# More tiles fetched row by row in a two-layer relational graph convolution: 119 instead of 95, with ScalarE taking part in layer 1

## The chip, the cores and the metric

The kernel runs on one core of a Trainium2 chip. The metric is device time in microseconds of one execution, as the median of several runs. The core has five engines with a queue each: TensorE (PE, with weight loads as PEld), VectorE (DVE), ScalarE (ACT), GpSimd (POOL) and SyncE (SP). DMAs are started here from the queues of SP, ACT and POOL.

## What is computed

12,500 nodes have 128 features each, and 200,000 edges, sorted by their target `dst`, have a source and one of eight types. A layer gives each node the sum over the types of the mean of its incoming messages of that type, adds the node's own product with `root` and a bias, and is followed by a relu and a residual. There are two such layers, and then a normalization of each row of `x + h`:

```python
W = jnp.einsum('rb,bio->rio', comp, basis)
xw = jnp.einsum('ni,rio->nro', x, W)
msgs = xw[src, et]
seg = dst * N_REL + et
mean = segment_sum(msgs, seg) / jnp.maximum(segment_sum(ones, seg), 1.0)[:, None]
agg = mean.reshape(N_NODES, N_REL, HIDDEN).sum(axis=1)
h_new = relu(agg + x @ root + bias)      # per layer; h = h_new + h
...
x = _layernorm(x + h, axis=-1)
```

## The kernel before

The edges are cut into 1563 tiles of 128, in the order of the targets; eight tiles make an octet, and there are 196 octets. Edge by edge, the row of the source has to come from HBM into a partition of its own: in layer 1 a row of `x` (512 bytes), in layer 2 a row of `y_d`, a table of every node's product with each of the eight type weights, which layer 1 writes as it goes (`table`, L1239; its stores are 512 KB each and leave from ACT's queue).

**How rows come.** Nearly every tile is fetched by one indirect DMA of POOL (`gather`, L687; the DMA is L707), which reads 128 rows by a column of indices. Seven octets of them fit into the ring `rows` (L558). `gathers` (L723) asks in iteration o for octet o + 5, and for the last six octets (`LATE`) only for octet o + 2, after PE has used the octet before (the `done` cell, L715). The other tiles, called lone here, are fetched by 128 plain DMAs of one row each, from SP's queue or ACT's (`lone_rows`, L641). These rows go in chunks of 32: one instruction loads 32 byte offsets into registers (L660), then 32 DMAs follow (L665). A chunk is due from 15 octets before its tile's octet (`EARLY`); SP issues in an iteration all that is due, ACT one chunk at most (the `break`, L671). The lists of lone tiles stand in L621 to L626: in layer 1 every 46th tile from 90 on by SP, 31 tiles; in layer 2 every 23rd from 44 on, by SP and ACT in turn, 32 tiles each. Layer 1's rows land in three buffers that are free by then (`jmp`, `comp_sb`, `sel`), layer 2's in four for each queue (the `sT` tiles); a chunk waits until PE has used the buffer's last tile. The byte offsets come from `load_offsets` (L675): two small loads on SP and three VectorE instructions in octet 1.

**What is done with them.** In layer 1, for each octet, VectorE builds one-hot matrices (`onehot`, L1030, line L1045), PE multiplies the rows by them (`means`, L1118, matmuls at L1128), ACT copies the result out (`take_means`, through `copy`, L608), PE multiplies by the weights (`product`) and places the result at its targets (`place`); between these, PE makes the table for layer 2, whose halves ACT copies out of PSUM (`y_row`, at L608). `batch` (L1419) gives ACT its work of an octet, right behind the octet's means. In layer 2, `add_rows` (L1278, matmuls at L1294) sums rows straight into blocks of 128 nodes. After every eight blocks `norm` (L1310) puts ten steps on a list, of which one is done per octet: turn, add x, statistics, a square root on ACT (L1347), scale, and a 512 KB store of the output on SP. When a block of eight begins its norm, the read of x for the block two further on, into the store's buffer, is put on the list behind the store (L1589), also on SP.

**What sets the order.** The program is a list of operations written out by hand, one loop iteration per octet. `Plan` turns reads and writes of named cells into semaphore waits. Each engine works through its own queue in order: a wait on SP or ACT holds everything behind it on that queue. A DMA into a buffer waits until the last reader and the last DMA of that buffer are done.

```python
while todo_ and todo_[0][0] // Q - EARLY <= q:
    t, j = todo_.pop(0)
    ...
    if e == "ACT":
        break
```

Of the kernel before, what the change touches and what calls it, by code (L numbers as in the profile page):

```python
# [422 lines left out]
def ordered_path(  # L423
# [25 lines left out]
    nc = tc.nc  # L449
# [28 lines left out]
    FIRST = 10  # L478
    TABLE = 50
    SOLO = 50  # L480
    ONE0, ONE_BY, CH, EARLY = 44, 23, 32, 15
    assert D == P and R * K == P and B == BF + 1 and 1 < TL and LAST < P and BF % 4 == 0 and Q == G and N % 2 == 0
    main = slice(HALO, HALO + P)

# [122 lines left out]
    def copy(out_t, in_t, reads, writes):  # L607
        act(lambda: nc.scalar.activation(out_t, in_t, AF.Copy), reads, writes)  # L608

    def in_turn(emits):  # L610
        def emit():
            for e in emits:
                last = e()
            return last

        return emit
# [1 line left out]
    rows_g = {}  # L618


    ones_at = list(range(ONE0, T - 8 * LATE - G, ONE_BY))  # L621
    single = [{t: ("SP", k) for k, t in enumerate(ones_at) if k % 2 == 0 and k > 0},
              {t: (("SP", "ACT")[k % 2], k) for k, t in enumerate(ones_at)}]
    turns_of = [{"SP": [], "ACT": []} for _ in range(L)]
    for l in range(L):
        for t in sorted(single[l]):  # L626
            turns_of[l][single[l][t][0]].append(t)
    offs = iota_f.bitcast(I32)
    byte = mybir.dt.uint8
    lone = {(0, "SP"): [(jmp.bitcast(F32), "jmp"), (comp_sb, "comp"), (sel.rearrange("p g k -> p (g k)"), "sel")]}  # L630
    for i, e in enumerate(("SP", "ACT")):
        f = sT_r.tiles[i].rearrange("p r g k -> p (r g k)")
        lone[1, e] = [(f[:, j * P:(j + 1) * P], ("sT", i, j // 4)) for j in range(4)]
    pending = {(l, e): [(t, j) for t in turns_of[l][e] for j in range(P // CH)] for l in range(L) for e in ("SP", "ACT")}

    def lone_tile(l, t):
        e, k = single[l][t]
        i = turns_of[l][e].index(t) % len(lone[l, e])
        return lone[l, e][i][0], [("lone", l, e, i, j) for j in range(P // CH)]

    def lone_rows(l, e, q):  # L641


        todo_ = pending[l, e]
        while todo_ and todo_[0][0] // Q - EARLY <= q:
            t, j = todo_.pop(0)
            k = single[l][t][1]
            o, cells = lone_tile(l, t)
            n = turns_of[l][e].index(t)
            writes = [cells[j]]  # L650
            if n < len(lone[l, e]) and j == 0:
                writes.append(lone[l, e][n][1])
            reads = [("offs", l)]
            if l == 1 and n == 0 and j == 0:
                reads += y_done
            table_b = (x if l == 0 else y_d).bitcast(byte).rearrange("n d -> (n d)")

            def emit(t=t, j=j, k=k, o=o):
                eng = nc.sync if e == "SP" else nc.scalar
                _, at = nc.values_load_multi_w_load_instructions(  # L660
                    offs[k:k + 1, l * P + j * CH:l * P + (j + 1) * CH],
                    engines=[mybir.EngineType.SP if e == "SP" else mybir.EngineType.Activation],
                    min_val=0, max_val=(N * (1 if l == 0 else R) - 1) * D * 4,
                    skip_runtime_bounds_check_because="the source of an edge is a node and its type a relation")
                return [eng.dma_start(o[j * CH + i:j * CH + i + 1, :].bitcast(byte),  # L665
                                      table_b[bass.ds(v, 4 * D)].rearrange("(p d) -> p d", p=1))
                        for i, v in enumerate(at)]

            plan.add(e, emit, reads, writes, lane="sr" if e == "SP" else "ar", n=CH)
            if e == "ACT":  # L670
                break  # L671
# [1 line left out]
    y_done = [("y_d", j) for j in range(NT - 2)] + [("y_d", j, k) for j in (NT - 2, NT - 1) for k in (0, 1)]  # L673

    def load_offsets():  # L675
        n = len(ones_at)
        for a, i in ((src, 0), (et, 1)):
            load(offs[:n, i * P:(i + 1) * P],
                 bass.AP(tensor=a.tensor, offset=a.offset + ONE0 * P, ap=[[ONE_BY * P, n], [1, P]]), [],
                 ["iota", ("offs", "raw", i)])  # L680
        a, b = offs[:n, :P], offs[:n, P:]
        vec(lambda: nc.vector.tensor_scalar(b, b, 4.0 * D, None, op0=ALU.mult), [], [("offs", "raw", 1)])
        vec(lambda: nc.vector.scalar_tensor_tensor(b, a, 4.0 * D * R, b, op0=ALU.mult, op1=ALU.add),
            [("offs", "raw", 0), ("offs", "raw", 1)], [("offs", 1)])
        vec(lambda: nc.vector.tensor_scalar(a, a, 4.0 * D, None, op0=ALU.mult), [], [("offs", "raw", 0), ("offs", 0)])

    def gather(l, q):  # L687
        if q >= NQ:
# [397 lines left out]
    def turn_x(n, h):  # L1086

        p, k = shape_of(n)
        pt, pc = pt_b
        m = min(4, k)  # L1090

        def first_step():
            t, c = xs[n]
            if h == 0:
                xT[n] = wide_r.take()

            def emit():
                for s in range(m):
                    last = nc.tensor.transpose(pt[:, s, :p], t[:p, 4 * h + s, :], ident[:p, :p])
                return last  # L1100

            pe(emit, [c, "ident"], [pc])

        def second_step():
            o, oc = xT[n]
            copy(by_slot(o, n)[:, 4 * h:4 * h + m, :], pt[:, :m, :p], [pc], [oc + (h,)])

        return first_step, second_step
# [9 lines left out]
    def means(o, half=None):  # L1118
        t, c = rows_g[0, o]
        d, dc = dms[0, o]  # L1120
        n = in_quad(o)

        lones = {i: lone_tile(0, o * Q + i) for i in range(n) if o * Q + i in single[0]}

        def some(i0, i1):
            def emit():
                for i in range(i0, i1):
                    last = nc.tensor.matmul(s_b[i // 4][0][:, i % 4, :], lones[i][0] if i in lones else t[:, i, :],  # L1128
                                            d[:, i, :], start=True, stop=True)
                return last  # L1130

            return emit

        if half is not None:
            pe(some(4 * half, 4 * half + 4), [c + (half,)] + dc, [s_b[half][1], ("done", 0)])
        else:
            pe(some(0, n), [c + (0,), c + (1,)] + dc + [x for _, cs in lones.values() for x in cs],
               [s_b[h][1] for h in range(-(-n // 4))] + [("done", 0)])
        plan.mark("PE")
# [99 lines left out]
    def table(j):  # L1239
# [5 lines left out]
        def half(k):  # L1245
            hb, bc = s_b[k] if j == NT - 2 else ct_b if split and k == 1 else pt_b

            def first_step():
                pe(lambda: nc.tensor.matmul(hb[:n].rearrange("p r d -> p (r d)"), hT[:, j * P:j * P + n],  # L1249
                                            w_sb[:, 1, k * H:(k + 1) * H, :].rearrange("p r d -> p (r d)"),  # L1250
                                            start=True, stop=True),
                   [("h", j)] + [("w", 1, r) for r in range(k * H, (k + 1) * H)], [bc])

            def second_step():
                if split and k == 1:
                    vec(lambda: nc.vector.tensor_copy(yr[:n, H:, :], hb[:n]), [bc], [yrc + (k,)])
                else:
                    copy(yr[:n, k * H:(k + 1) * H, :], hb[:n], [bc], [yrc + (k,)])
                if split:
                    load(y_d[j * P * R:(j * P + n) * R, :].rearrange("(p r) d -> p r d", r=R)[:, k * H:(k + 1) * H, :],  # L1260
                         yr[:n, k * H:(k + 1) * H, :], [yrc + (k,)], [("y_d", j, k)])
                elif k == 1:
                    stores.append(lambda: load(
                        y_d[j * P * R:(j * P + n) * R, :].rearrange("(p r) d -> p (r d)", r=R),
                        yr[:n].rearrange("p r d -> p (r d)"), [yrc + (0,), yrc + (1,)], [("y_d", j)], "ACT"))

            return first_step, second_step
# [10 lines left out]
    def add_rows(q, k, opens, last):  # L1278
# [8 lines left out]
            more += [hc, ("w", 1, R)]  # L1287

        lones = {i: lone_tile(1, q * Q + i) for i in range(n) if q * Q + i in single[1]}

        def some(i0, i1):
            def emit():
# [155 lines left out]
    for o in range(NG - 3):  # L1448
# [11 lines left out]
        onehot(0, o + 2, o - 1)  # L1460
        if parts is None:
            run(later, 1)
        if not opened:
            end()
        for step in opened:
# [19 lines left out]
        for i in range(2):  # L1485
# [4 lines left out]
            else:  # L1490
                break
            while copies:
                copies.pop(0)()
            a()
            if b is not None:
                copies.append(b)
# [69 lines left out]
    for q in range(NQ):  # L1566
# [15 lines left out]
        for i in range(2):  # L1582
            for j, step in ending:
                step()
                n = j // S
                if j >= 0 and (j % S == S - 1 or j == NT - 1):
                    norm(n)
                    if n + 2 < NX:
                        todo.append(lambda n=n: load_x(n + 2))  # L1589
            ending.clear()  # L1590
            if i == 0 and last:
                a, b = finish(1, k)
# [64 lines left out]
```

## Time and profile before

| What | us |
|---|---|
| median of 3 runs (lowest, highest) | 3869.61 (3868.55, 3869.77) |
| the profiled execution | 3870.23 |
| its span, first to last instruction | 3868.4 |
| layer 1, first to last gather of POOL | 4.3 to 1933.5 |
| layer 2, first to last gather of POOL | 1952.8 to 3848.6 |
| POOL busy, 3039 instructions | 2878.4 |
| PE busy | 2329.0 |
| VectorE busy | 1648.0 |
| ScalarE busy | 392.6 |

The span is 1.8 us shorter than the time of the execution that it belongs to. "Busy" leaves out the DMA issues and register loads of SP and ACT: SP never shows as busy, and ACT's share (10%) doesn't hold its single-row DMAs. Those are seen in the rows with "SPq" or "ACTq", in the list of DMA issues, and as packets of the DMA queues: q0 is POOL's gathers, q1 is SP's DMAs, q10 is ACT's. The chain of work that ended last goes back from the last instruction to whatever released each wait; an engine with a large share there is one that the end depended on.

### The profile page before, as it was taken

What the parts mean: (1) busy time and instruction counts of PE and PEld (TensorE: products, weight loads), DVE (VectorE), ACT (ScalarE), POOL (GpSimd) and SP (SyncE); (2) the same over time, 40 slices, a digit from 0 to 9 for tenths busy, and PEclk for the clock granted to TensorE, in tenths of its full rate; (3) what the DMA queues carried; (4) which work ended last, traced back from release to release, by engine and by line L of the source; (5) the groups of instructions that cost most, each with busy time, mean ns of one, the idle gap of its engine ahead of it and who ended that gap; (6) DMA issues with size and microseconds to landing.
All of it is one profiled execution on the core that took longest, in us unless ns stands there. A gap on an engine that the chain in (4) does not pass through costs nothing.

```text
span 3868.4 us, 57003 instructions
## 1 busy us (share of the span) xinstructions
PE 2329.0 (60%) x11213; PEld 1881.1 (49%) x11213; DVE 1648.0 (43%) x4646; ACT 392.6 (10%) x838; POOL 2878.4 (74%) x3039
## 2 busy tenths in 40 slices
PE   6767677777766676767755555555444354353446
PEld 4655555555555565655534444444334243242334
DVE  6654443333334333333233444443544353453445
ACT  1111112222111121221200000000000000000000
POOL 7777777777777777777767777777777777777775
PEclk8989889888888888888877777777777686776777
DMA  4122133333222222222222222222222222222222
GB/s 122 52 59 59 54 98 98 114 103 108 90 86 82 87 87 82 87 83 86 90 76 55 56 56 66 61 61 67 61 61 67 55 67 55 64 59 59 66 53 67
DMA packets 151007, 286.26 MB, mean 74 GB/s; under 512 B 64591, under 2 KB 84315, under 8 KB 150643
## 3 DMA queue, kind: packets, MB, share of 16 engines
q0 software_dynamic: 96992, 198.83, 19.9%
q10 hardware_dynamic: 25065, 54.12, 4.1%
q1 hardware_dynamic: 28586, 29.58, 2.8%
q14 instruction: 273, 2.24, 0.2%
q8 instruction: 91, 1.49, 0.2%
HBM read 223.63 MB, written 58.65 MB: 73 GB/s over the span
## 4 chain that ended last, share of the span: by engine, by line
POOL 47%; issue 19%; SPq 18%; DMA 7%; PE 5%; DVE 3%; ACT 0%; POOLq 0%; ACTq 0%; DVEq 0%
POOL rows L707 47%; SPq L665 14%; DMA rows<-y_d,idy 4%; SPq L660 4%; DMA out_dram<-x_g 2%; DVE dm L1045 2%; PE s L1294 1%; PE s L1128 1%; PE y L1160 1%; DVE arena L864 1%; DMA sT<-y_d 0%; PE ct L874 0%; PE ct L875 0%; PE ct L1294 0%; DMA rows<-in_x_dram,idx 0%
## 5 line engine op out<-in xcount | busy, mean ns | idle before, releaser
L707 POOL DMA_INDIRECT rows<-in_x_dram,idx x1532 | 1462.2, 954 | 469.3 <-issue 465.1
L707 POOL DMA_INDIRECT rows<-y_d,idy x1499 | 1415.1, 944 | 500.0 <-issue 446.7
L1045 DVE TENSOR_SCALAR dm<-cols,near,w 128x256 f32<-128x256 f32 x1563 | 723.7, 536 | 935.4 <-PE s L1294 515.1
L1294 PE MATMUL s<-dm,rows 128*128 128x256 f32 x2000 | 583.0, 447 | 422.9 <-DMA sT<-y_d 232.0
L1045 DVE TENSOR_SCALAR dm<-cols,kr,w 128x128 f32<-128x128 f32 x1563 | 526.7, 403 | 624.6 <-PE s L1128 460.3
L1128 PE MATMUL s<-dm,rows 128*128 128x128 f32 x3064 | 532.6, 343 | 410.1 <-DMA rows<-in_x_dram,idx 409.3
L1128 PEld LDWEIGHTS s<-dm,rows 128*128 128x128 f32 x3064 | 490.8, 250 | 526.4 <-DMA rows<-in_x_dram,idx 513.0
L1294 PEld LDWEIGHTS s<-dm,rows 128*128 128x128 f32 x2000 | 441.8, 229 | 531.5 <-issue 375.1
L1294 PE MATMUL ct<-dm,rows 128*128 128x256 f32 x998 | 308.2, 468 | 353.2 <-DMA sT<-y_d 177.5
L1294 PEld LDWEIGHTS ct<-dm,rows 128*128 128x128 f32 x998 | 232.3, 242 | 412.1 <-issue 310.3
L1160 PE MATMUL y<-w_sb,sT 128*128 128x128 f32 x1968 | 282.3, 304 | 44.3 <-ACT sT L608 44.3
L1160 PEld LDWEIGHTS y<-w_sb,sT 128*128 128x128 f32 x1968 | 270.8, 220 | 54.4 <-ACT sT L608 53.3
L608 ACT ACTIVATE sT<-s 128x512 f32<-128x512 f32 x391 | 213.4, 605 | 287.6 <-PE s L1128 287.6
L1249 PE MATMUL pt<-w_sb,arena 128*128 128x512 f32 (+1 forms) x386 | 203.4, 609 | 40.5 <-ACT y_row L608 39.2
L1209 DVE TENSOR_TENSOR v<-po,carry 128x128 f32<-128x128 f32 x98 | 28.5, 290 | 465.6 <-PE s L1128 279.7
L608 ACT ACTIVATE y_row<-pt 128x512 f32<-128x512 f32 x195 | 116.5, 597 | 1026.2 <-PE s L1128 902.0
L1347 ACT ACTIVATE st<-st,eps 128x8 f32<-128x8 f32 (+1 forms) x13 | 4.0, 308 | 1612.8 <-DMA sT<-y_d 1385.6
L1160 PE MATMUL ct<-w_sb,sT 128*128 128x128 f32 (+1 forms) x1168 | 164.5, 301 | 0.9 <-ACT sT L608 0.7
L1160 PEld LDWEIGHTS ct<-w_sb,sT 128*128 128x128 f32 (+1 forms) x1168 | 161.3, 220 | 1.7 <-ACT sT L608 1.7
L1191 PE MATMUL po<-pl,ys 128*128 128x256 f32 x392 | 126.8, 405 | 6.1 <-ACT sT L608 1.4
L1249 PEld LDWEIGHTS pt<-w_sb,arena 128*128 128x128 f32 (+1 forms) x386 | 63.0, 190 | 91.9 <-ACT y_row L608 87.9
L1053 DVE TENSOR_SCALAR pl<-cols,pos 128x256 f32<-128x256 f32 x196 | 93.3, 477 | 0.0
(151 smaller groups left out, 1077.3 us busy)
## 6 DMA issues: line engine op xcount, KB each, us to landing
sT<-y_d SPq DMA_DIRECT2D x4096, 0.5 KB
sT<-y_d ACTq DMA_DIRECT2D x4096, 0.5 KB
y_d<-y_row ACTq DMA_DIRECT2D x96, 512.0 KB
rows<-in_x_dram,idx POOLq DMA_INDIRECT x1532
rows<-y_d,idy POOLq DMA_INDIRECT x1499
jmp<-in_x_dram SPq DMA_DIRECT2D x1408, 0.5 KB
comp_sb<-in_x_dram SPq DMA_DIRECT2D x1280, 0.5 KB
sel<-in_x_dram SPq DMA_DIRECT2D x1280, 0.5 KB
```

The lines of the kernel that those rows point to most:

```text
L608: act(lambda: nc.scalar.activation(out_t, in_t, AF.Copy), reads, writes)
L660: _, at = nc.values_load_multi_w_load_instructions(offs[k:k + 1, l * P + j * CH:l * P + (j + 1) * CH], engines=[mybir.EngineType.SP if e = ...
L665: return [eng.dma_start(o[j * CH + i:j * CH + i + 1, :].bitcast(byte), table_b[bass.ds(v, 4 * D)].rearrange("(p d) -> p d", p=1)) for i, v ...
L707: ins.append(nc.gpsimd.indirect_dma_start(out=t[:, i - q * Q, :], out_offset=None, in_=x if l == 0 else y_d, in_offset=bass.IndirectOffset ...
L864: one = (lambda s=s, eq=eq, s0=s0: nc.vector.tensor_tensor(eq[:, s - s0, :nb, HALO - s:HALO + P], key[:, :nb, HALO - s:HALO + P], key[:, : ...
L1045: emits.append(lambda i=i: nc.vector.tensor_scalar(t[:, i - q * Q, :wide], cols[:, :wide], ids[:, i:i + 1], w[:, i:i + 1], op0=ALU.is_equa ...
L1053: emits.append(lambda: nc.vector.tensor_scalar(o[:m], cols[:m], pos[:m, g // (2 * R), g % (2 * R):g % (2 * R) + 1], None, op0=ALU.is_equal))
L1128: last = nc.tensor.matmul(s_b[i // 4][0][:, i % 4, :], lones[i][0] if i in lones else t[:, i, :], d[:, i, :], start=True, stop=True)
L1160: last = nc.tensor.matmul(y[:m], t[:, r, :nt, :].rearrange("p t k -> p (t k)"), w_sb[:, 0, r, :], start=(r == 0), stop=(r == R - 1))
L1191: ins = nc.tensor.matmul(a, o[:m], t[:m], start=opens, stop=last and not root_in)
L1249: pe(lambda: nc.tensor.matmul(hb[:n].rearrange("p r d -> p (r d)"), hT[:, j * P:j * P + n], w_sb[:, 1, k * H:(k + 1) * H, :].rearrange("p ...
L1294: ins = nc.tensor.matmul(a, lones[i][0] if i in lones else t[:, i, :], d[:, i, :], start=(opens and i == 0), stop=(last and i == n - 1))
```

## The change

The lists of lone tiles are written anew. Each queue has a first tile and a step for each layer, up to the end of octet 193. Layer 1 gets 34 tiles on SP (from 90, every 43rd) and 17 on ACT (from 498, every 64th); layer 2 gets 35 on SP (from 50, every 43rd) and 33 on ACT (from 53, every 46th). That is 119 tiles, and 3007 gathers of POOL are left of 3031.

- ACT's rows in layer 1 go 16 at a time, one chunk per octet, from 10 octets ahead of their tile. They are issued behind the octet's `batch`, once the preparation in `parts` is over. They land in two buffers in `mixer`.
- `load_offsets` now loads the two layers' offsets separately, six small loads instead of two, with `comp_sb` as a helper buffer for the types, and three VectorE instructions over other partitions.
- Where two copies fall into one octet of layer 1, the first is done by VectorE (`vcopy`) and not by ACT.
- The read of x in layer 2 comes four octets behind the output's store in the list of steps, where it came one octet behind.

```diff
-    ONE0, ONE_BY, CH, EARLY = 44, 23, 32, 15
+    EARLY = 15
...
+    def vcopy(out_t, in_t, reads, writes):
+        vec(lambda: nc.vector.tensor_copy(out_t, in_t), reads, writes)
...
-    ones_at = list(range(ONE0, T - 8 * LATE - G, ONE_BY))
-    single = [{t: ("SP", k) for k, t in enumerate(ones_at) if k % 2 == 0 and k > 0},
-              {t: (("SP", "ACT")[k % 2], k) for k, t in enumerate(ones_at)}]
+    LONES = (("SP", 90, 43), ("ACT", 62 * Q + 2, 8 * Q)), (("SP", 50, 43), ("ACT", 53, 46))
+    rows_at_once = {(0, "SP"): 32, (0, "ACT"): 16, (1, "SP"): 32, (1, "ACT"): 32}
...
+            ts = range(t0, (NQ - 2) * Q, by)
...
+    mixer_f = mixer.rearrange("p m k -> p (m k)")
+    lone[0, "ACT"] = [(mixer_f[:, j * P:(j + 1) * P], "mixer") for j in range(2)]
...
-        todo_ = pending[l, e]
-        while todo_ and todo_[0][0] // Q - EARLY <= q:
+        todo_, CH = pending[l, e], rows_at_once[l, e]
+        while todo_ and todo_[0][0] // Q - (10 if (l, e) == (0, "ACT") else EARLY) <= q:
...
     def load_offsets():
...
+        ty = comp_sb.bitcast(I32)
+        for l in range(L):
+            for p, t0, by, n in lists[l]:
+                for a, o, c in ((src, offs[:, l * P:(l + 1) * P], ["iota", ("offs", "raw", l)]),
+                                (et, ty, ["comp", ("offs", "ty")]))[:l + 1]:
+                    load(o[p:p + n, :], bass.AP(tensor=a.tensor, offset=a.offset + t0 * P, ap=[[by * P, n], [1, P]]),
+                         [], [c[0], c[1] + (p,)])
...
         if parts is None:
             run(later, 1)
+            lone_rows(0, "ACT", o)
...
             while copies:
-                copies.pop(0)()
+                copies.pop(0)(vcopy)
...
                     if n + 2 < NX:
-                        todo.append(lambda n=n: load_x(n + 2))
+                        todo.extend([lambda: None] * 3 + [lambda n=n: load_x(n + 2)])
```

More of the change, by code (lines that the diff above doesn't have):

```diff
@@ L618, in ordered_path @@
     rows_g = {}
-    ones_at = list(range(ONE0, T - 8 * LATE - G, ONE_BY))
-    single = [{t: ("SP", k) for k, t in enumerate(ones_at) if k % 2 == 0 and k > 0},
-              {t: (("SP", "ACT")[k % 2], k) for k, t in enumerate(ones_at)}]
-    turns_of = [{"SP": [], "ACT": []} for _ in range(L)]
+    LONES = (("SP", 90, 43), ("ACT", 62 * Q + 2, 8 * Q)), (("SP", 50, 43), ("ACT", 53, 46))
+    rows_at_once = {(0, "SP"): 32, (0, "ACT"): 16, (1, "SP"): 32, (1, "ACT"): 32}
+    single, turns_of, lists = [], [], []
     for l in range(L):
-        for t in sorted(single[l]):
-            turns_of[l][single[l][t][0]].append(t)
+        single.append({})
+        turns_of.append({})
+        lists.append([])
+        for e, t0, by in LONES[l]:
+            ts = range(t0, (NQ - 2) * Q, by)
+            lists[l].append((len(single[l]), t0, by, len(ts)))
+            turns_of[l][e] = list(ts)
+            for t in ts:
+                assert t not in single[l]
+                single[l][t] = e, len(single[l])
+        assert len(single[l]) <= P
     offs = iota_f.bitcast(I32)
@@ L633, in ordered_path @@
         lone[1, e] = [(f[:, j * P:(j + 1) * P], ("sT", i, j // 4)) for j in range(4)]
-    pending = {(l, e): [(t, j) for t in turns_of[l][e] for j in range(P // CH)] for l in range(L) for e in ("SP", "ACT")}
+    pending = {(l, e): [(t, j) for t in turns_of[l][e] for j in range(P // rows_at_once[l, e])] for l in range(L) for e in ("SP", "ACT")}
     def lone_tile(l, t):
         e, k = single[l][t]
+        assert not pending[l, e] or pending[l, e][0][0] >= t
         i = turns_of[l][e].index(t) % len(lone[l, e])
-        return lone[l, e][i][0], [("lone", l, e, i, j) for j in range(P // CH)]
+        return lone[l, e][i][0], [("lone", l, e, i, j) for j in range(P // rows_at_once[l, e])]
     def lone_rows(l, e, q):
-        todo_ = pending[l, e]
-        while todo_ and todo_[0][0] // Q - EARLY <= q:
+        todo_, CH = pending[l, e], rows_at_once[l, e]
+        while todo_ and todo_[0][0] // Q - (10 if (l, e) == (0, "ACT") else EARLY) <= q:
             t, j = todo_.pop(0)
@@ L675, in load_offsets @@
     def load_offsets():
[L676 to L685, printed above, removed]
+        ty = comp_sb.bitcast(I32)
[5 more added lines that the diff above has]
+                         [], [c[0], c[1] + (p,)])
+        n0, n = len(single[0]), len(single[1])
+        a, b, ty = offs[:n0, :P], offs[:n, P:], ty[:n, :]
+        raw = [[("offs", "raw", l, p) for p, _, _, _ in lists[l]] for l in range(L)]
+        tys = [("offs", "ty", p) for p, _, _, _ in lists[1]]
+        vec(lambda: nc.vector.tensor_scalar(a, a, 4.0 * D, None, op0=ALU.mult), [], raw[0] + [("offs", 0)])
+        vec(lambda: nc.vector.tensor_scalar(ty, ty, 4.0 * D, None, op0=ALU.mult), [], tys)
+        vec(lambda: nc.vector.scalar_tensor_tensor(b, b, 4.0 * D * R, ty, op0=ALU.mult, op1=ALU.add),
+            ["comp"] + tys, raw[1] + [("offs", 1)])
     def gather(l, q):
@@ L1102, in first_step, with second_step @@
             pe(emit, [c, "ident"], [pc])
-        def second_step():
+        def second_step(copy=copy):
             o, oc = xT[n]
@@ L1123, in means @@
         lones = {i: lone_tile(0, o * Q + i) for i in range(n) if o * Q + i in single[0]}
+        assert not any(p and p[0][0] < o * Q + n for p in (pending[0, "SP"], pending[0, "ACT"]))
         def some(i0, i1):
@@ L1252, in first_step, with second_step @@
                    [("h", j)] + [("w", 1, r) for r in range(k * H, (k + 1) * H)], [bc])
-            def second_step():
+            def second_step(copy=copy):
                 if split and k == 1:
@@ L1289, in add_rows @@
         lones = {i: lone_tile(1, q * Q + i) for i in range(n) if q * Q + i in single[1]}
+        assert not any(p and p[0][0] < q * Q + n for p in (pending[1, "SP"], pending[1, "ACT"]))
         def some(i0, i1):
```

## The prediction

> **What bounds the kernel now.** I read the chain of work that ended last, then the costliest groups, then the waits, then the DMA queues by stretches.
>
> ```profile
> POOL 47%; issue 19%; SPq 18%; DMA 7%; PE 5%; DVE 3%; ACT 0%; POOLq 0%; ACTq 0%; DVEq 0%
> ...
> L707 POOL DMA_INDIRECT rows<-in_x_dram,idx x1532 | 1462.2, 954 | 469.3 <-issue 465.1
> L707 POOL DMA_INDIRECT rows<-y_d,idy x1499 | 1415.1, 944 | 500.0 <-issue 446.7
> ```
>
> Two engines carry the chain: POOL, which issues a gather for nearly every tile, and SyncE's queue (SPq), which fetches the other tiles row by row. A gather of POOL costs 0.944 us and 0.305 us of issue: in layer 1 between 1000 and 1800 us, 640 of them filled 799.9 us, 1.249 us each. So a tile taken from POOL is worth 1.249 us, as long as POOL is what ends last.
>
> In layer 1 it is: POOL goes at that pace from 4.3 to 1933.5 us, and PE ends an octet's means 4 to 5 us behind the octet's last gather. In layer 2 (1952.8 to the end) it is only just so. POOL waits 25.4 us for PE from 3150 us on, because PE waits for rows:
>
> ```profile
> POOL rows L707 <- PE ct L1294: 13.4, 3, 5.5
> POOL rows L707 <- PE s L1294: 12.0, 4, 5.0
> ```
>
> The rows are what has no room in layer 2. Both issuing queues work without a break from its start nearly to its end (4096 rows each; times are of the first and last issue):
>
> ```profile
> L665 SPq DMA_DIRECT2D sT<-y_d x4096: 227/228/604, 1954.2 to 3771.7; - x196
> L665 ACTq DMA_DIRECT2D sT<-y_d x4096: 234/235/618, 1954.3 to 3706.0; - x196
> ```
>
> What limits them? SyncE's own waits show 115.9 us behind the output's store, which the change removes:
>
> ```profile
> SPq L605 <- DMA out_dram<-x_g: 115.9, 9, 16.4
> ```
>
> But the DMA queues say that issuing is not the limit. q1 is SyncE's, q10 ScalarE's; a row is two packets, 512 bytes and 4 bytes. First 2120 to 2320 us, in which SyncE doesn't stop, then 2327 to 2343 us, in which it waits for a store:
>
> ```profile
> q1 hardware_dynamic: 921, 0.24, 1.6%
> q10 hardware_dynamic: 891, 0.23, 1.2%
> ```
> ```profile
> q1 hardware_dynamic: 203, 0.54, 11.0%
> q10 hardware_dynamic: 69, 0.02, 1.0%
> ```
>
> The first pair is 906 rows in 200 us, **4.53 rows/us** for both queues together (2.30 and 2.23). In the second, less the store's 128 packets of 4 KB, it is 72 rows in 16 us, 4.5 rows/us, although SyncE issued none: a backlog was served. Early in the layer (1956 to 2056 us) 252 and 249 rows are issued and 466 moved, so the backlog grows, to some 12 us of rows in each queue; then an issue takes up to 604 ns instead of 227. When ScalarE is done (3710 to 3770 us), SyncE alone moves 354 packets, 2.95 rows/us. So the two queues share one pace, and SyncE's stops are mostly covered by what is queued.
>
> [...]
>
> **The change, part by part.** Base: the profiled execution, 3870.2 us with a span of 3868.4; the median of the runs, 3869.61, is 0.6 us less.
>
> *Fewer gathers.* Layer 1 goes from 31 single-row tiles to 34 + 17 = 51, layer 2 from 64 to 35 + 33 = 68. POOL issues 20 and 4 gathers less: 20 x 1.249 = **-25.0 us** and -5.0 us where POOL ends last.
>
> *Layer 2's rows.* There are 68 x 128 = 8704 of them, not 8192. With SyncE no longer stopped, both queues stay at the shared pace: ScalarE needs 4224 / 2.23 = 1894 us, a few less for the faster start (466 rows per 100 us), say 1890. SyncE has moved 2.30 x 1890 = 4347 by then; the other 133, at its lone issue pace (154 rows in 60 us), take 52 us. Its last row is issued some 1940 us after its first; before, that took 3771.7 - 1954.2 = 1817.5. Its last tile, 1512, lies in octet 189, and the gathers of octets 192 to 195 wait for PE to have used it: 27 x 1.249 = 34 us, 5 us for landing and matmuls, and 3868.4 - 3848.6 = 20 us from the last gather to the end. So layer 2 lasts about 1940 + 59 = 1999 us from its first row, against 3868.4 - 1954.2 = 1914: +85. It is less if both queues end together at the pace of the whole layer: by 3700 us some 8030 rows were out in 1746 us, 4.60/us, so 8704 / 4.60 + 59 = 1951, +37. POOL, held up, also leaves the DMAs freer: where it issued 37 gathers in 50 us (3360 to 3410), 475 row packets were moved, 4.75 rows/us. I take **+75**, near the upper end, because ScalarE's share can't pass to SyncE before it ends.
>
> *The read of x, three octets later.* The store and the load have 4 chunks of 32 rows between them in SyncE's queue, over 50 us, so the nine stops go. Cover: the next block's sum needs that read an interval of 16 octets later (turns at 2312 and 2468 us). Nothing else stands behind it but rows. Its worth at a shared pace is 0 to -10 us (the pace falls from 4.53 to about 4.3 for 40 us around a store); taken as 0, inside the +75.
>
> *ScalarE's 16 rows an octet in layer 1.* From octet 52 on, an octet lasts (8 - 0.31) x 1.249 = 9.6 us. ScalarE's work in it: copies 1.75 us (1200.04 to 1201.78), a table store 0.34, 16 rows at 249 per 100 us with their load, 6.4, or up to 7.6 if the register load stays at 2.26 us for half the rows (one register takes 0.46). Sum 8.5 to 9.7: it just fits, or loses 0.1 x 130 octets = 13 us, within the 55 us between PE's last use of a rows buffer and the gather that fills it again (octet 184's means end at 1834.7 us, octet 191's gather starts at 1890.0). The queued work behind it is the next `take_means`, for which PE waits; a delay stays in that room until it is used up.
>
> *Layer 1's rows together.* SyncE: 128 per 43 tiles, 41.3 x 1.249 = 51.6 us, 2.48/us; ScalarE 16 / 9.6 = 1.67/us; 4.15 together, under 4.53, but with 96 table stores of 512 KB on ScalarE's queue. A SyncE tile took 53 us in 518 to 1262 us, against 51.6: it loses 1.5 us a tile over 25 tiles, 37 us. Its lead at 518 us, with nine tiles fetched: the tenth, 477 in octet 59, would be there at 571 us, and PE is at octet 56 at 579.7, three octets short, so at 609: 38 us. That is used up at the end. Bounds: 0 to +60. I take **+5**.
>
> *The small ones.* Some 76 copies (62 of `y_row`, 14 of `wide`, those that made ScalarE wait for PE inside an octet) go to VectorE: 0.6 to 1.1 us each beside a VectorE that is idle over half of layer 1 and waits for the same matmuls; 0. Were that cover gone, 76 us at most. Four more loads of offsets on SyncE at 2 us each (45.90 to 49.88 us for the two now) hold VectorE and the first rows by 8 us in octet 1, where POOL's ring has room (octet 2's means end at 63.8 us, octet 9's gather starts at 97.0); 0.
>
> **Sum**: 3870.2 - 25 + 5 + 75 = 3925 us. Layer 2's four gathers give nothing, since POOL isn't last there.
>
> **Rivals.**
> *Faster.* SyncE's stops, not the pace, hold layer 2. Then 140 chunks of 12.7 us (its pace right after a stop, 2343 to 2420) are 1780 us, POOL ends last, its 25 us of waits go too: 3870.2 - 25 - 5 - 23 = **3817**. For it: the nine stops lie on the chain. It decides at 4.8 rows/us: 8704 rows by octet 189's gathers, 1453 x 1.249 = 1815 us. Against: 4.53 to 4.75 in every stretch, stops included. Anything between ends about level.
> *Slower still, layer 1.* The pace binds there too, as the stores take DMA time: SyncE at 2.30 rows/us needs 55.7 us a tile, 25 x 4.1 = 103 us behind demand, less 38 of lead: +65 in place of +5, **3985**. For it: from 520 us on SyncE has at most 38 us of lead and must now win none. Against: x's rows were fetched alone without a sign of backlog.
> [...]
> *The change doesn't do what it says*: the read still finds the store unfinished. Then SyncE stops 116 us in sum and ends up to 40 us later, near 3960.
>
> **Chances.** Forecast 0.56, layer 1 binding too 0.15, stops remaining 0.05; faster 0.20; level 0.04. Within 0.2% (8 us, about what a measurement of this kernel can tell from no change): 0.04; faster 0.20; slower 0.76. The range, 3850 to 3985, leaves out about 0.14 below and 0.05 above; the slower cases alone lie within 3890 to 3985.
>
> **What would show it.** Right: POOL's gathers 3007 at 944 ns, but some 75 us or more of waits for PE in layer 2; no wait of SPq for `out_dram<-x_g`; SPq's rows of `sT` ending about 100 us nearer the layer's end; packets of q1 and q10 at 4.5 to 4.75 rows/us through layer 2, 906 to 950 per 200 us; layer 1 ending near 1910 to 1915 us. Wrong: more than 4.8 rows/us, or POOL without waits in layer 2 (then the faster rival); POOL waiting for PE before 1900 us (then layer 1's).

## The result, and the profile after

| | before, us | after, us |
|---|---|---|
| median (lowest, highest), 4 runs each | 3869.08 (3868.18, 3869.77) | 3911.43 (3910.33, 3913.71) |
| the profiled execution, its span | 3870.23, 3868.4 | 3911.06, 3908.9 |
| layer 1, first gather to end of the last | 4.3 to 1933.5 | 4.6 to 1908.0 |
| layer 2, first gather to the end of the span | 1915.6 | 1984.1 |
| POOL's waits for PE in layer 2 | 26.9 | 103.5 |

The ratio is 1.011 (95%: 1.0093 to 1.0128): the change makes the kernel slower, by 42 us where 55 were forecast. The experiments fell on several chips, which differ: on one of them, called A below, the kernel before takes 3869.65 us, as it does here; on the four others, called B, it takes 5757 to 5833 us. Which chip the table's runs had is not on record; since their times for the kernel before are 0.6 us apart, they are compared with chip A's. Each experiment is compared with runs of the kernel before on its own chip.

The page's chain of work that ended last, and its two largest groups (busy us, mean ns of one | idle before, and what ended most of it):

```profile
POOL 35%; SPq 31%; issue 19%; ACTq 6%; PE 4%; DMA 2%; DVE 2%; ACT 1%; POOLq 0%; DVEq 0%
...
L726 POOL DMA_INDIRECT rows<-y_d,idy x1495 | 1411.2, 944 | 570.6 <-issue 440.2
L726 POOL DMA_INDIRECT rows<-in_x_dram,idx x1512 | 1442.4, 954 | 463.7 <-issue 458.3
```

A gather takes what it took, 944 ns, and there are 3007. But the chain has moved to SyncE's queue: its share goes from 18% to 31%, and POOL's falls from 47% to 35%. In layer 2 POOL now idles 570.6 us, of which only 440.2 lie between gathers.

The two row queues in layer 2, from the list of DMA issues by line (ns min/median/max; first and last issue):

```profile
L679 SPq DMA_DIRECT2D sT<-y_d x4480: 227/228/632, 1926.7 to 3849.2; - x195
L679 ACTq DMA_DIRECT2D sT<-y_d x4224: 234/235/597, 1926.8 to 3781.2; - x192
```

SyncE issues its last row 1922.5 us after its first, and the span ends 59.7 us later; before, it was 1817.5 us. SyncE hardly stops meanwhile. Its own waits from 1920 us on, and POOL's there (us in total, times, longest):

```profile
SPq L605 <- DMA out_dram<-x_g: 5.3, 1, 5.3
```
```profile
POOL rows L726 <- PE s L1315: 79.0, 14, 14.9
POOL rows L726 <- PE ct L1315: 24.5, 5, 8.2
```

The nine stops behind the output's store, 115.9 us, are gone, as the change means them to be, and the queue ends later all the same. Why the end depends on that queue is seen in the last part of the chain in order of time (start, duration, what):

```profile
3836.95 2.10 SPq L674
3849.16 1.18 DMA sT<-y_d
3850.47 1.19 PE s L1315 x2
3851.66 0.43 PE s L1318 x2
3852.09 4.10 PE s L1315 x14
3856.45 0.94 POOL rows L726
```

SyncE loads the last 32 offsets at 3837, its last row lands at 3850, PE uses the tile, and only then may POOL gather the last four octets: 27 gathers and 20 us, to 3908.9.

Last, the DMA queues from 2120 to 2320 us (packets, MB, share of 16 engines):

```profile
q1 hardware_dynamic: 1064, 0.76, 2.3%
q10 hardware_dynamic: 892, 0.23, 1.2%
```

q1 holds 128 packets of a 512 KB block besides the rows. Without them it is 936 + 892 packets, 914 rows in 200 us, 4.57 rows/us; in the same stretch it was 906 before. The pace did not rise.

### The profile page after: what moved, and what is told of

It reads as the page before. It is cut to its first block, busy times and chain, and to the rows that moved or that the text cites. A ratio compares the mean times of both kernels' runs of the same rounds, so it can differ in the third digit from the quotient of the medians.

```text
span 3908.9 us, 63322 instructions
## 1 busy us (share of the span) xinstructions
PE 2252.7 (58%) x11213; PEld 1811.6 (46%) x11213; DVE 1684.7 (43%) x4714; ACT 346.9 (9%) x770; POOL 2854.7 (73%) x3015
## 4 chain that ended last, share of the span: by engine, by line
POOL 35%; SPq 31%; issue 19%; ACTq 6%; PE 4%; DMA 2%; DVE 2%; ACT 1%; POOLq 0%; DVEq 0%
POOL rows L726 35%; SPq L679 24%; SPq L674 6%; ACTq L679 5%; ACTq L674 1%; PE s L1148 1%; DMA rows<-y_d,idy 1%; DVE dm L1064 1%; PE s L1315 1%; PE y L1180 1%; DMA rows<-in_x_dram,idx 1%; ACT sT L608 1%; PE ct L893 0%; DVE arena L883 0%; PE ct L894 0%
## 5 line engine op out<-in xcount | busy, mean ns | idle before, releaser
L726 POOL DMA_INDIRECT rows<-y_d,idy x1495 | 1411.2, 944 | 570.6 <-issue 440.2
L726 POOL DMA_INDIRECT rows<-in_x_dram,idx x1512 | 1442.4, 954 | 463.7 <-issue 458.3
L1315 PE MATMUL s<-dm,rows 128*128 128x256 f32 x2004 | 566.3, 437 | 619.0 <-DMA sT<-y_d 365.7
L1315 PEld LDWEIGHTS s<-dm,rows 128*128 128x128 f32 x2004 | 430.3, 223 | 723.0 <-issue 443.7
L1148 PE MATMUL s<-dm,rows 128*128 128x128 f32 x3024 | 496.5, 328 | 295.9 <-DMA rows<-in_x_dram,idx 286.5
L1148 PEld LDWEIGHTS s<-dm,rows 128*128 128x128 f32 x3024 | 458.7, 237 | 413.5 <-DMA rows<-in_x_dram,idx 372.2
L1315 PE MATMUL ct<-dm,rows 128*128 128x256 f32 x986 | 277.4, 434 | 294.3 <-DMA sT<-y_d 162.7
L1315 PEld LDWEIGHTS ct<-dm,rows 128*128 128x128 f32 x986 | 210.7, 222 | 345.7 <-issue 246.0
L1269 PE MATMUL pt<-w_sb,arena 128*128 128x512 f32 (+1 forms) x386 | 215.5, 642 | 45.9 <-DVE y_row L611 43.9
L611 DVE COPY y_row<-pt 128x512 f32<-128x512 f32 x56 | 38.7, 692 | 356.8 <-PE pt L1269 356.8
L608 ACT ACTIVATE y_row<-pt 128x512 f32<-128x512 f32 (+1 forms) x139 | 83.0, 597 | 1047.9 <-PE s L1148 669.6
L1211 PEld LDWEIGHTS po<-pl,ys 128*128 128x128 f32 x392 | 62.8, 195 | 136.1 <-ACT sT L608 129.2
```

Of the source, the lines that this page charges most:

```text
L611: vec(lambda: nc.vector.tensor_copy(out_t, in_t), reads, writes)
L726: ins.append(nc.gpsimd.indirect_dma_start(out=t[:, i - q * Q, :], out_offset=None, in_=x if l == 0 else y_d, in_offset=bass.IndirectOffset ...
L1211: ins = nc.tensor.matmul(a, o[:m], t[:m], start=opens, stop=last and not root_in)
L1315: ins = nc.tensor.matmul(a, lones[i][0] if i in lones else t[:, i, :], d[:, i, :], start=(opens and i == 0), stop=(last and i == n - 1))
```

## The experiments

**ScalarE's rows of layer 2 given back to POOL (chip A).**

```diff
-(("SP", 50, 43), ("ACT", 53, 46))
+(("SP", 50, 43), ("ACT", 9999, 46))
```

> The kernel after, with ScalarE's 33 single-row tiles of layer 2 given back to POOL (1528 gathers there, not 1495); layer 1 is unchanged. Theory (one shared pace for both row queues, and layer 2 too full for it): SP's 4480 rows alone ask for 4480 / 1908 = 2.35 rows/us, under the 4.6 that both reached together, so a chunk takes the 12.6 to 12.8 us of its issue and not the 13.7 it took in the kernel after; SP's last row then comes 140 x 12.7 = 1780 us after its first, POOL ends last and its waits for PE in layer 2 fall from some 98 us to under 30. Layer 2 lasts 1528 x 1.249 = 1908 us and the 40 around it; where the kernel before takes 3869 us this gives 3870 to 3885, faster than the kernel after although ScalarE's help is taken away. Rival (POOL's waits come from the block ends, with ScalarE's late square root, and not from the rows): the waits stay near 98 us, and the 33 gathers more add 41 us: 3950. On a chip where the kernel before takes some 5825 us, a tile by rows cost about 21 us of the queue against 1.25 us for a gather: SP alone then needs 140 chunks at 20 us or more, 2800 us in layer 2, near the 2925 that it took with both queues, since a chunk lost its time there to the gathers and not to the other queue.

Measured: 3856.55 us against 3869.65 for the kernel before, ratio 0.9967 (0.9954 to 0.9979). It beats both kernels. That is below the 3870 to 3885 us expected, but the theory's own terms, 1908 us of gathers from 1928.8 us on and 20 us behind them, add up to 3857: the expectation added them wrongly. Its chain, its group of layer 2's gathers, its row queue (from the list by line), its waits of POOL from 1920 us on, and q1 from 2120 to 2320 us:

```profile
POOL 66%; issue 22%; PE 4%; ACTq 4%; DVE 2%; DMA 2%; ACT 1%; POOLq 0%; SPq 0%; DVEq 0%
...
L729 POOL DMA_INDIRECT rows<-y_d,idy x1528 | 1442.8, 944 | 484.9 <-issue 465.8
```
```profile
L680 SPq DMA_DIRECT2D sT<-y_d x4480: 227/228/364, 1930.3 to 3730.8; - x195
```
```profile
POOL rows L729 <- issue: 465.8, 1527, 0.3
POOL rows L729 <- DMA y_d<-y_row: 19.2, 1, 19.2
```
```profile
q1 hardware_dynamic: 1144, 0.78, 1.2%
```

The same 4480 rows of SyncE take 1800.5 us instead of 1922.5, 12.9 us a chunk (12.6 to 12.8 were expected) and not 13.7, only because ScalarE issues none. In 200 us SyncE moves (1144 - 128) / 2 = 508 rows, 2.54/us, where it moved 468 beside ScalarE. The packets tell how. Taken from the trace by size, a row's 512-byte packet in these 200 us takes 25.7 ns on average; in the kernel after it takes 91.1 ns in q1 and 72.3 ns in q10, with a median of 27 ns against 25 here. So most packets go nearly as fast as alone (361 of q1's 460 in the kernel after take at most 30 ns), and others take far longer (88 of them 300 ns or more). POOL has no wait for PE left in layer 2, SPq is off the chain, and 33 more gathers, 41 us, make the span 52.4 us shorter. So ScalarE's 33 tiles cost layer 2 some 94 us and saved 41. What the rival says, that the late square root holds PE, the time of this run can't exclude: without its rows ScalarE takes the square root at once, and VectorE's wait for it falls from 245.1 us to 0.7. The two traces can, for SyncE's queue. Added up, its 4480 issues take 1029 us here and 1151 us in the kernel after, while the loads of offsets into registers (311 us) and the register move ahead of each issue (130 us in sum) are the same in both. The 122 us between the sums are the whole 122 us by which the queue ended later. Where something else held SyncE's queue, as the output's store did in the kernel before, the trace lists waits, 115.9 us of them; in layer 2 of the kernel after it lists 10 us in sum, and the issues are longer.

**Hardly any row tiles (chip A).**

```diff
-LONES = (("SP", 90, 43), ("ACT", 62 * Q + 2, 8 * Q)), (("SP", 50, 43), ("ACT", 53, 46))
+LONES = (("SP", 90, 700), ("ACT", 9999, 64)), (("SP", 50, 700), ("ACT", 9999, 46))
```

> The kernel after with only three single-row tiles in each layer (SP: 90, 790, 1490 and 50, 750, 1450), all others gathered by POOL: 3120 gathers, not 3007. Theory (a gather costs 1.249 us of POOL wherever nothing else is late): where the kernel before takes 3869 us, 3120 - 3031 = 89 gathers more than before, 111 us, less the 25 us of waits that POOL had in layer 2: 3955 to 3985, slower than the kernel after by 45 to 75 us. On a chip where the kernel before takes some 5825 us the theory says that row issues are held up by POOL's gathers, so without them it is POOL's pace alone: also 3955 to 4000, a third faster than the kernel before there. Rival for such a chip (everything is slow there, not the row issues alone): POOL's gathers would fall behind as well, and the time stays well over 5000 us.

Measured: 3953.25 us, ratio 1.0217 (1.02 to 1.0234), just under the range expected. From the list by line:

```profile
L729 POOL DMA_INDIRECT rows<-y_d,idy x1560: 940/944/1095, 1984.1 to 3931.1; - x195
L729 POOL DMA_INDIRECT rows<-in_x_dram,idx x1560: 940/944/1762, 4.4 to 1964.7; - x195
```

POOL alone sets the time: 1560 gathers in 1947 us in layer 2. Against the kernel after, layer 1's last gather starts 1964.7 - 1907.1 = 57.6 us later for 48 gathers, 1.20 us each: that is what a row tile is worth in layer 1. So row tiles do pay on chip A, as long as the queues can carry them; this kernel is 42 us slower than the kernel after, and 97 slower than the one with SyncE's rows alone in layer 2.

**The change in its two halves (chips B).** Layer 1's new lists alone, with layer 2's lists and the read of x as before; and layer 2's new lists with the later read, with layer 1's lists and copies as before. The layer that is as before also gets its old end of the list (not shown); `load_offsets` stays as changed in both:

```diff
-(("SP", 50, 43), ("ACT", 53, 46))
+(("SP", 44, 46), ("ACT", 67, 46))
...
-todo.extend([lambda: None] * 3 + [lambda n=n: load_x(n + 2)])
+todo.append(lambda n=n: load_x(n + 2))
```
```diff
-(("SP", 90, 43), ("ACT", 62 * Q + 2, 8 * Q))
+(("SP", 90, 46), ("ACT", 9999, 64))
...
-copies.pop(0)(vcopy)
+copies.pop(0)()
```

> The changed kernel with layer 2's lists and its read of x as they were before (64 tiles in layer 2), layer 1 as changed. If the two queues' shared pace of rows is what layer 2 lost by, layer 1 keeps its 25 us and layer 2 is as before: 3844 us. If layer 1's new rows delay something that only shows in layer 2, the time is above 3860.

> Layer 1 as before (31 tiles, copies on ScalarE), layer 2 as changed. Shared pace: 8704 rows at 4.6 per us, the whole loss of layer 2 and none of layer 1's gain, 3937 us. If the loss needs both layers' changes, below 3900.

Measured, against 5832.78 us for the kernel before on that chip: layer 1 alone 6066.25, ratio 1.0401 (1.0383 to 1.0419); layer 2 alone 5916.39, ratio 1.0147 (1.013 to 1.0164). This answers another question than it was made for. Layer 1's 20 row tiles with their copies, a gain of 25 us in the kernel after's profile, are a loss of 233 us here, 12 us a tile. It lies in layer 1: POOL's last gather there starts at 2882.8 us with the new lists and at 2651.4 with the old ones. On this chip few rows are issued while POOL gathers. From the trace of layer 1's half, within layer 2, 20 us in which POOL issues one gather, and 12 us in which it issues nine (queues: packets, MB, share; then issues):

```profile
q10 hardware_dynamic: 104, 0.03, 0.6%
q1 hardware_dynamic: 98, 0.03, 0.5%
...
sT<-y_d ACTq DMA_DIRECT2D x53, 0.5 KB
sT<-y_d SPq DMA_DIRECT2D x52, 0.5 KB
rows<-y_d,idy POOLq DMA_INDIRECT x1
```
```profile
q0 software_dynamic: 320, 0.66, 20.9%
q1 hardware_dynamic: 8, 0.00, 0.1%
q10 hardware_dynamic: 8, 0.00, 0.1%
...
rows<-y_d,idy POOLq DMA_INDIRECT x9
sT<-y_d SPq DMA_DIRECT2D x5, 0.5 KB
sT<-y_d ACTq DMA_DIRECT2D x5, 0.5 KB
```

That is 105 rows in 20 us, 5.25/us, without gathers, and 10 rows in 12 us, 0.8/us, beside them. Without gathers a packet takes 16 ns: 98 packets are 0.5% of 16 engines for 20 us. What is slow beside the gathers is the issuing itself, 5 rows of each queue in 12 us.

**The read of x put back (chips B).** The edit is the second hunk of the first diff above, alone; it ran on two chips.

> The changed kernel with the read of x one octet behind the store again, so that SyncE stops for the store. Shared pace: the stops are covered by the backlog; 3911 to 3921 us although some 100 us of SPq waits for out_dram<-x_g come back. If SyncE's own issue time is what layer 2 ends by, the stops add nearly all of themselves: about 4000 us.

> The changed kernel with the read of x one octet behind the store again, on another chip than e3. Where the kernel before takes about 3870 us: shared pace, the stops are covered by the backlog, 3911 to 3921 us although some 100 us of SPq waits for out_dram<-x_g come back. If SyncE's own issue time is what layer 2 ends by, the stops add nearly all of themselves: about 4000 us.

Measured: 6173.54 us, ratio 1.0575 (1.0554 to 1.0596), and 6152.93, ratio 1.0581 (1.0546 to 1.0616). The stops that the edit was to bring back hardly come: SyncE waits for the store 24.2 us in the first run and 22.8 in the second, ten times each, not some 100. So neither hypothesis is tested here. The kernel after itself was not run on these chips either, so what the later read is worth isn't measured by itself; the two halves of the change, 4.0% and 1.5%, add up to about the same.

**Wider steps in layer 2 (chips B).** 64 tiles, as many as before, on three chips:

```diff
-(("SP", 50, 43), ("ACT", 53, 46))
+(("SP", 50, 48), ("ACT", 53, 48))
```

> The changed kernel with layer 2's tiles at every 48th on both queues (32 + 32 tiles, 8192 rows, up to tile 1541). Shared pace: one tile of each queue per 48 is 256 rows per 57.5 us, 4.45 per us, just under the pace, so POOL ends last through layer 2 without waits: 1499 gathers, 3815 us. If ScalarE's late square roots hold layer 2 (245 us of VectorE waits for st, 108 before), they remain, and the time stays above 3850.

> The changed kernel with layer 2's tiles at every 48th on both queues (32 + 32 tiles, 8192 rows, up to tile 1541), on another chip than e4. Where the kernel before takes about 3870 us: shared pace, 256 rows per 57.5 us are 4.45 per us, just under the pace, so POOL ends last through layer 2 nearly without waits for PE: 3815 us. If ScalarE's late square roots hold layer 2 (245 us of VectorE waits for st, 108 before), they remain, and the time stays above 3850.

> The same kernel as in the two runs with wider steps before (layer 2 with 32 + 32 tiles, every 48th on each queue, 8192 rows as in the kernel before; the rest as after), now asked of a chip where the kernel before takes 3869 us. Theory: layer 1's 20 gathers fewer are worth their 25 us; layer 2's 8192 rows need 8192 / 4.6 = 1781 us, and its 1499 gathers 1872, so the rows fit: POOL waits under 30 us in layer 2, which lasts some 1883 us from its first gather to the last, and the time is 3830 to 3850. Rival (layer 2 is slower because of the later read of x or the offsets, not because of the number of rows): it stays above 3890.

Measured: 6020.3, 5999.21 and 5996.82 us, ratios 1.0321 (1.0293 to 1.0348), 1.0317 (1.0283 to 1.0351) and 1.0326 (1.029 to 1.0363). Fewer row tiles in layer 2 are better here than the change's 68, by 2.5% against the kernel with the read put back on the same chips, which differs from it in the read as well, but layer 1's loss stays. For chip A, where the question was asked, this says nothing; the third run was to answer it and didn't.

**Without the square root (chips B).**

```diff
-            act(lambda: nc.scalar.activation(st[:p, :k, A + M], st[:p, :k, A + 1], AF.Sqrt, bias=eps[:p]),
-                [sc + (1,), "eps"], [sc + (2,)])
...
-nc.vector.reciprocal(st[:p, :k, A + M], st[:p, :k, A + M]), [sc + (2,)], [sc + (3,)])
+nc.vector.reciprocal(st[:p, :k, A + M], st[:p, :k, A + 1]), [sc + (1,)], [sc + (3,)])
```

> The kernel after without the square root of the normalization (the reciprocal is taken of the variance itself, and eps is left out), so that VectorE no longer waits for ScalarE at the ends of the blocks; the output is therefore not the normalized one. All 119 single-row tiles stay. Theory (the two row queues share one pace, which layer 2 exceeds): VectorE's 245 us of waits for the square root go, but PE still waits for rows of sT, POOL for PE by some 90 to 100 us, and the time stays within 10 us of the 3911 of the kernel after. Rival (the late square root, queued behind ScalarE's rows, is what delays PE and with it POOL in layer 2): POOL's waits fall under 40 us, and the time comes to 3850 to 3870, like that of the kernel in which ScalarE had no rows.

> The same kernel without the square root once more, asked of a chip where the kernel before takes 3869 us. Theory (the two row queues share one pace, which layer 2 exceeds): VectorE's waits for the square root go, PE still waits for rows of sT, SP's last row comes 1900 to 1925 us after its first, and the time is 3900 to 3915, the kernel after's. Rival (the late square root is what delays PE and with it POOL): 3850 to 3870.

Measured: 6129.86 us, ratio 1.0569 (1.0538 to 1.06), and 6159.97, ratio 1.0574 (1.0548 to 1.0599), level with the kernel with the read put back, which ran on two other chips B and has the square root, but the earlier read. POOL's waits for PE in layer 2 are 1153 us in the second run, against 1172 and 1134 there, and didn't fall. On these chips, then, the late square root makes no difference that shows. For chip A it remains untried.

**Layer 2 by POOL, layer 1 as after (a chip B).**

```diff
-(("SP", 50, 43), ("ACT", 53, 46))
+(("SP", 50, 700), ("ACT", 9999, 46))
```

> The kernel after with layer 2's single-row tiles cut from 68 to three (SP: 50, 750, 1450), the rest gathered by POOL (1560 gathers there, not 1495); layer 1 as after. Theory (in layer 2 the rows set the end, and a gather costs 1.249 us): where the kernel before takes 3869 us, layer 2's gathers need 1560 x 1.249 = 1948 us from their start at 1925, and the end comes 20 us behind: 3885 to 3900, faster than the kernel after's 3911 although no row tile helps POOL, since 65 tiles by rows cost there more than they save. Rival (the kernel after's 98 us of waits in layer 2 are not due to the rows): the waits stay, and the time is 3960 or more. On a chip where the kernel before takes some 5820 us, row issues go on there at 0.5 to 1 per us beside gathers; theory for such a chip: layer 1 stays as slow as it was (2870 us) and layer 2 falls from some 3100 us to 1990, 4850 to 4950 in all, 0.83 to 0.85 of the kernel before. Rival there (the whole chip is slower, whatever the rows do): layer 2 stays above 2700 us, and the time above 5600.

Measured: 5102.88 us against 5757.11, ratio 0.8861 (0.8833 to 0.8888). Layer 2's gathers here, and, for comparison, gathers and SyncE's rows in the second run without the square root, from the lists by line:

```profile
L729 POOL DMA_INDIRECT rows<-y_d,idy x1560: 938/944/1062, 2835.7 to 5067.4; - x195
```
```profile
L726 POOL DMA_INDIRECT rows<-y_d,idy x1495: 938/944/999, 2920.4 to 6126.2; - x187
```
```profile
L679 SPq DMA_DIRECT2D sT<-y_d x4480: 2/228/1433, 2922.3 to 6086.5; - x195
```

65 gathers more, and the layer's gathers take 2232 us, not 3206: 974 us less, 15 us for every row tile taken out. The second kernel ran on another chip B; on this one, the kernel with the read put back took 3230 us for them, which gives 15 us as well. The theory's direction holds, but not its size: 1990 us were expected. POOL's 1560 gathers at 1.249 us are 1948; of the 284 us more, most are waits of POOL, 275 us in sum or some 1.4 us an octet, for which the trace names no releaser (it calls them `remote`). So on chips B the rows are most of what makes layer 2 long, and not all.

## Why the prediction was right, and where its sizes were off

Forecast: slower, 3925, as the sum 3870.2 - 25 + 5 + 75. Measured in the profiled execution: 3868.4 - 25.5 (layer 1) - 2.5 (the gap between the layers, 19.3 to 16.8) + 68.5 (layer 2) = 3908.9. The forecast was 14 us too slow: 5 for layer 1's rows, 6.5 for layer 2's, and 2.5 for the gap, which no term of it foresaw.

- **Layer 1's gathers, -25.0:** -25.5. POOL waits for PE 2.7 us in all before 1905 us. The kernel with hardly any row tiles gives 1.20 us a tile for 48.
- **Layer 1's rows, +5 (0 to +60):** 0. The rival in which the pace binds in layer 1 too is refuted on chip A; the 4.15 rows/us that were reckoned for both queues there cost nothing. What makes the two queues share a pace no view shows: a row is one data packet (461 of 512 bytes in q1 for SyncE's 463 issues, 2120 to 2320 us, before), and which engine carries it isn't told.
- **ScalarE's 16 rows an octet, 8.5 to 9.7 of 9.6 us:** they fit. The layer's pace shows no loss.
- **Layer 2's rows, +75 (+37 to +85):** the term that was mis-sized, by 6.5. The pace over the whole layer was 4.60 rows/us: up to ScalarE's last row, 1854.4 us after the first, 4311 + 4224 rows are out (SyncE issues 2.49/us after that). Counted in the same way it was 4.58 in the kernel before. The prediction put both queues at the 4.53 of one stretch, and so ScalarE's end at 1890 and SyncE's at 1940; they came at 1854 and 1922.5. The tail was reckoned at 59 and is 59.7. POOL's waits for PE came to 103.5 us, 76.6 more than before; some 75 or more were named as the sign. Another sign, that SyncE's rows end about 100 us nearer the layer's end, did not fit the prediction's own sum (its last row 122 us later, the layer 85 longer); they ended 37 us nearer, 59.7 before it and not 96.7.
- **SyncE's stops, 0 to -10, taken 0:** the faster rival held that these bind. They fell from 115.9 to 5.3 us, the queue never idled, and it ended later. A chunk took 13.7 us, not the 12.7 that the rival needed. Where the gain went is seen in the two paces up to ScalarE's last row: SyncE's rose from 2.24 to 2.32 rows/us, and ScalarE's fell from 2.34 to 2.28. The run with SyncE alone shows the same: the time of a row depends on what the other queue issues (SyncE moves 2.54 rows/us alone and 2.34 beside ScalarE, 2120 to 2320 us). That the stops alone are worth nothing on chip A was not tried by itself.
- **The small ones, 0:** 68 copies go to VectorE, not 76 (56 of `y_row` at 692 ns each, 12 of `wide` at up to 1073 ns); layer 1 shows no cost or gain beyond its gathers. The offsets show none either.

A cause that the prediction did not weigh is the square root behind ScalarE's rows; VectorE's waits for it went from 108.4 to 245.1 us:

```profile
DVE st L1372 <- ACT st L1368: 245.1, 10, 46.3
```

Against it as what sets the end: SyncE's queue, which the end followed, waited only 10 us in sum in layer 2, and its longer issues account for the whole 122 us that ScalarE's rows cost it, so nothing that PE or VectorE do late can have moved its last row by much. That is read from the traces; no run on chip A leaves out the square root alone.

What the second issuing queue brings is seen on chip A from 2120 to 2320 us: 2.54 rows/us for one queue and 4.57 for two. The second queue moves 2.23 and takes 0.2 from the first. So one queue alone, as it issues here, leaves the second something to bring, up to the 4.6 of this kernel; no run shows more than that over a whole layer on chip A.

Fewer row tiles than the change's and more than SyncE's alone might be faster than 3856.55 us on chip A. By the traces 8192 rows fit into 8192 / 4.60 = 1781 us, against 1499 x 1.249 = 1872 of gathers; the kernel that would show it ran on chips B alone.

## What to carry to other kernels

Before work is moved to an idle queue, count what that queue and its neighbour move together, and over the whole stage: two queues of single-row transfers can be at their shared pace although one of them shows waits (4.53 rows/us here, with 115.9 us of waits over the layer), and taking a wait away need not bring the end forward (here 5.3 us of them were left, and the queue ended 105 us later). The queue that is at its pace should carry no more than fits beside the engine that it relieves (here 8704 rows were too many, 4480 were not), because what it ends late is paid at the end, once its lead is used up (its last row came 105 us later, the layer got 68.5 us longer). And a balance tuned on one chip is a property of that chip: here a row tile gained 1.2 us on one and cost 12 to 15 on another.

## What the runs showed of the hardware that was not expected

- On chips B, SyncE and ScalarE issue rows at 5.25/us while POOL issues one gather in 20 us and at 0.8/us while it issues nine in 12; a single issue of layer 2 takes up to 1.4 us there (1433 ns in the row above, against 632 in the kernel after's profile), with the median unchanged at 228 ns. The register move ahead of an issue, which transfers nothing, takes up to 1411 ns in the same run and 29 in the median (29 throughout layer 2 of the kernel after), so it is the queue's instructions that stand still and not its transfers. A gather still takes 944 to 947 ns. What stops them isn't settled. Eight traces of chips B also hold `remote` waits, VectorE's above all (1579 us in the run with layer 2 by POOL); in the four of the kernel before, the kernel after and chip A none is seen.
- On one of those chips a kernel with 54 row tiles in place of 119 or 95, all but three in layer 1, takes 5102.88 us, 11% less than the kernel before.
- On chip A a row's 512-byte packet takes about three times as long on average (72 to 91 ns and not 26) when the second queue issues rows too, with the median at 27 ns and not 25, and at nearly the same number of rows per us in the first queue (2.34 and not 2.54).
